# Issuing the last exchange's first round ahead of a residual load, and a bias addition after its second round

## The chip, the core and the metric

The kernel runs on one core of a Trainium2 chip. The metric is device time in microseconds for one execution. TensorE (PE) multiplies matrices, VectorE (DVE), ScalarE (ACT) and GpSimd (POOL) do element-wise work, SyncE (SP) issues DMAs; GpSimd and ScalarE issue some too. Each engine takes its own instructions in order and waits at semaphores for the others.

## The reference, cut to what matters

Eight sequences of 512 tokens by 512 features go through attention with 16 heads of 32, whose queries and keys are shifted by a condition's projections; the input is added to the result.

```python
Q = _split_heads(x @ Wq.T + bq); K = ...; V = ...      # x: (8, 512, 512), 16 heads of 32
tQ = _split_heads(tokens @ Wq.T + bq); tK = ...        # tokens: the condition, one row a sequence
cQ = Q + tQ; cK = K + tK
scores = jnp.einsum('bhqd,bhkd->bhqk', cQ, cK) / jnp.sqrt(jnp.float32(HEAD_DIM))
attn = jax.nn.softmax(scores, axis=-1)
out = jnp.einsum('bhqk,bhkd->bhqd', attn, V)
return x + out.transpose(0, 2, 1, 3).reshape(B, S, D_MODEL)
```

## The kernel before

**Steps.** A step `t` is one sequence (`t // 4`) and four of its heads (`t % 4`), so there are 32, numbered 0 to 31. Work of neighbouring steps is interleaved by hand; nothing reorders it. The framework only adds the semaphore waits that the data need, and it gives the DMAs of SyncE eight semaphores in turn, so that a DMA also waits until the one eight places ahead of it has landed.

**One step.** Scores are computed twice. With queries along the partitions they give the row maxima (VectorE) and, by ScalarE's exponentials, the row sums. With keys along the partitions, and the maxima taken off by a product, they give exponentials that TensorE can multiply with V. For the steps 1 to 29 (`KEPT`) the second form is computed for half of the queries alone. For the other half the exponentials of the first form are kept (`kept[t]`, in the big buffer `store`) and turned: VectorE transposes their 32x32 blocks (`turn_kept`, L660), and then the blocks off the diagonal change places between the four groups of 32 partitions. That is the exchange, `swap_kept(t, move)`, with six pairs of blocks and three rounds of six DMAs of 128 KB:

```python
to, of = [(aside, part(a, g)), (part(a, g), part(g, a)), (part(g, a), aside)][move]
...
(nc.gpsimd if here else nc.sync).dma_start(to, of)     # L682
```

Round 0 copies one block of a pair aside, round 1 moves the other block into its place, round 2 brings the first back. So a pair's round 1 waits for its round 0 to land, and its round 2 for its round 1. For step 29, the last exchange, SyncE issues all of round 0 and the first three pairs of rounds 1 and 2; GpSimd issues the last three pairs of rounds 1 and 2. The prediction calls them first, second and third round. `times_v_half(t, kc, 0, ...)` multiplies the exchanged blocks with V (L840).

**The residual.** `load_residual(t)` issues four DMAs on SyncE (L190), each 64 KB in rows of 32 numbers, into `xr[t]`. `bias_residual(t)` adds V's bias on GpSimd (L203). In `send(t, ...)` VectorE transposes the step's output, GpSimd multiplies by the reciprocals (L913) and adds `xr[t]` (L914), and SyncE stores it (L917).

**The place in the program.** The loop over `thirds(t)` runs up to `t = 28`; in its second third it loads the residual of step 29 and issues that step's first round. Code without a loop follows for steps 29, 30 and 31: the first part, for `t = 29`, holds the second and third round, the row sums' masks (`masked`, L865), the loading of the residual of step 30, and the biases of step 29 and 31. (The last step's residual is already in the core, as `xT`.) Then come the exponentials of step 29's other half, and with `t = 30` `crossed(t, kc, qc)`: scores of step 31 for maxima (L641), maxima and scores of step 30 (L1302, L1305), exponentials on ScalarE (L1320), reductions on VectorE (L1322, L650). After the first `crossed` stands the product of step 29's exchanged blocks, `halves_of(t - 1, banks(2), (0,))`, into a bank that the exponentials of that `crossed` have just emptied; after the second and third stand parts of step 30's own product (`times_v`, L824).

Of the kernel before, what the change touches and what calls it, by code (L numbers as in the profile page):

```python
# [17 lines left out]
def kernel(  # L18
# [112 lines left out]
    def begin(*ws):  # L131
        for w in ws:
            rows = order[w : w + 4]
            pairs = [(j, j + 1) for j in rows if j + 1 in rows]
            last = max(
                pairs, key=lambda p: rows.index(p[0]) + rows.index(p[1]), default=sorted(rows[2:])
            )
            order[w : w + 4] = [j for j in rows if j not in last] + list(last)
        row_of[0] = list(order)
# [22 lines left out]
    def spread(a, d):  # L162

        return a.rearrange("(f j) d -> j f d", j=BL)[:, :, d : d + BL]
# [12 lines left out]
    def turned_by_vector(t):  # L177

        return t < T - 1

    def load_residual(t):

        b, g = divmod(t, G)
        if turned_by_vector(t):
            if t == T - 2:
                xr[t] = late[0][:, 2, :].rearrange("p (f e) -> p f e", e=BL)
            else:
                xr[t] = op.tile([P, NB, BL], F32, tag="xr", name=f"xr_{t}")
            for h in range(HG):
                nc.sync.dma_start(  # L190
                    xr[t][h * BL : (h + 1) * BL], spread(x[b], g * P + h * BL)
                )
        else:

            xr[t] = xT[b][:, g, :]

    def bias_residual(t):

        if turned_by_vector(t):
            bias = bvs[:, t % G, :].unsqueeze(1).broadcast_to([P, NB, BL])  # L200
        else:
            bias = bvl.broadcast_to([P, S])
        nc.gpsimd.tensor_tensor(xr[t], xr[t], bias, ALU.add)  # L203
# [393 lines left out]
    def row_max(t, qc, hold=False, w=HG, scores=True):  # L597

        if t >= T:
            return  # L600
        open_max(t)
        for j in range(HG if scores else 0):
            row_scores(t, qc, j, banks(w + j))
        if row_of[0] or t < T - 2 or t * NS + qc == T * NS - 1:
            for j in range(2) if scores else (1, 0):
                one_max(t, qc, j, banks(w + j))
        else:
            row_max_of(t, qc, 0, banks(w, 2))
        last, both = [banks(w + 2), banks(w + 3)], banks(w + 2, 2)
        apart = row_of[0] and row_of[0][w + 3] - row_of[0][w + 2] > 1  # L610

        def held():
            if apart or hold and t < T - 2:
                for j in range(2):
                    one_max(t, qc, 2 + j, last[j])
            else:
                row_max_of(t, qc, 1, both)

        if hold:
            return held  # L620
        held()
        return nothing
# [4 lines left out]
    def row_max_aside(t, qc):  # L627

        open_max(t)
        for j in range(HG):  # L630
            row_scores(t, qc, j, banks(j))
        nc.scalar.copy(spare, banks(0).rearrange("p (c f) -> p c f", f=P))  # L632
        for j in (1, 2, 3):
            one_max(t, qc, j, banks(j))

    def max_aside(t, qc):
        nc.vector.tensor_reduce(nmax[t][:, qc, 0:1, 0], spare, AX.XY, ALU.max, negate=True)
# [27 lines left out]
    def swap_kept(t, move, some=range(6)):  # L665

        later = 6 if t % 4 == 1 else 2

        def part(a, g):
            return kept[t][a * BL : (a + 1) * BL, g].rearrange("p c h s -> p (c h s)")  # L670

        for n in some:
            a, g = APART[n]
            at = (n + 2) % HG * BL
            aside = (store[:, 6:8] if t == KEPT[-1] else between)[at : at + BL, n // HG]
            aside = aside.rearrange("p i s -> p (i s)")
            to, of = [(aside, part(a, g)), (part(a, g), part(g, a)), (part(g, a), aside)][move]
            if t < KEPT[-1]:
                here = move == 2 or move == 0 and n >= later
            else:  # L680
                here = move > 0 and n >= 3
            (nc.gpsimd if here else nc.sync).dma_start(to, of)  # L682
# [205 lines left out]
    def weighted(t, pt, pd, between):  # L888

        apart = masked(t)
        if t in KEPT:
            of = (0, 2, 1, 3)
            for half in (1, 0):
                for kc in of:
                    times_v_half(t, kc, half, pt, of)
                if half == (t + 1 not in KEPT):
                    spread_sums(apart, pd)
        else:  # L900
            for kc in range(NS):
                times_v(t, kc, pt)
                if kc == (NS - 1 if t + 1 in KEPT else 0):
                    spread_sums(apart, pd)
        rec = reciprocals(t, pd)
        between()
        send(t, pt, rec)
# [237 lines left out]
    def turn_more(t, i, after):  # L1145

        for _ in range((TURNED if t + 1 < KEPT[-1] else TURNED_LAST).get((i, after), 0)):
            if t + 1 in KEPT:
                n = turned[t + 1] = turned.get(t + 1, -1) + 1
                turn_kept(t + 1, n)  # L1150
        even = t % 2 == 0
        if (i, after) == ((2, 1) if even else (0, 2)) or (t, i, after) == (2, 0, 2):
            turn_x(next_x[0])
            next_x[0] += 1

    def thirds(t, made):

        b, r = divmod(t, G)
        of = (t - 1) // G + 1
        begin(0, HG)  # L1160
        turn_more(t, 0, 0)
        row_max_aside(t + 1, 1)
        max_aside(t + 1, 1)
        row_max(t + 1, 2, False, HG)
        turn_more(t, 0, 1)
        denominators(t + 1, 1, None, (1, 2, 3, 0))
        denominators(t + 1, 2, HG)
        weighted(t - 1, banks(0), banks(1), nothing)
        turn_more(t, 0, 2)
        load_blocks(1)  # L1170
        one_item(of, *next(made), (2, 3), ignore, nothing)
        released(0, 1, 4, 5, 7, 6, 2, 3)
        for i in (1, 2):
            begin(HG)
            rows = (t + 1, 3) if i == 1 else (t + 2, 0)
            if i == 1:
                joined(t, i - 1, rows)
                turn_more(t, i, 0)
                row_max(*rows, False, HG, False)
            else:  # L1180
                exponentials_of_rest(t, i - 1)
                turn_more(t, i, 0)
                row_max(*rows, False, HG)
            turn_more(t, i, 1)
            if i == 1:
                first = range(6 if t + 1 < KEPT[-1] else 3)
                swap_kept(t, 2, first)
                split_max(t + 1)
                turn_max(t + 1)
                swap_kept(t, 2, range(len(first), 6))  # L1190
            dens = lambda js=range(HG): denominators(*rows, HG, js)
            n, u, kind = next(made)
            if kind == "first":
                products(of, n, u, kind, False, dens, nothing, None)
                turn_more(t, i, 2)
            elif n == "v":
                small = nothing
                if t + 1 not in KEPT:
                    small = lambda: transpose_max(t + 1, banks(2), nc.scalar.copy)
                other_shared(of, n, u, dens, (0, 3), small, lambda: turn_more(t, i, 2))  # L1200
                released(1, 2, 4, 5, 6, 7, 0, 3)
            else:
                products(of, n, u, kind, False, dens, nothing, False)
                turn_more(t, i, 2)
            if i == 1:
                aparts[t] = masked(t)
            if (t + 1, i) == (KEPT[-1], 1):
                load_residual(t + 1)
                swap_kept(t + 1, 0)
            if i == 2:  # L1210
                if r == 0:
                    combine_x(b + 1, 1, nc.gpsimd)
            else:
                if t > 1:
                    bias_residual(t)
                if r == 0:
                    combine_x(b + 1, 0, nc.gpsimd)
            if i == 2 and t + 1 < KEPT[-1]:
                swap_kept(t + 1, 0)
                load_residual(t + 1)  # L1220
                swap_kept(t + 1, 1)
# [105 lines left out]
    t = T - 3  # L1327
# [11 lines left out]
    else:  # L1339
        row_max_of(t + 1, 2, 1, banks(HG + 2, 2))  # L1340
    row_max_of(t + 1, 2, 0, late[0][:, :2, :])
    bias_residual(t)
    swap_kept(t, 1)
    apart = masked(t - 1)
    aparts[t] = masked(t)
    load_residual(t + 2)
    bias_residual(t + 2)
    swap_kept(t, 2)
    load_residual(t + 1)
    halves_of(t - 1, banks(0), (1,))  # L1350
# [23 lines left out]
    t = T - 2  # L1374
# [25 lines left out]
    t = T - 1  # L1400
# [101 lines left out]
```

## Time and profile before

| what | value |
|---|---|
| median of 3 runs | 649.97 us (649.82 to 650.51) |
| span of the profiled execution | 648.4 us |
| full time of the profiled execution | not given |
| busy: TensorE, VectorE, ScalarE, GpSimd | 99%, 93%, 82%, 63% of the span |
| DMAs within `store` issued by SyncE | 264 of 128 KB, median 2.7 us to landing |
| DMAs within `store` issued by GpSimd | 258 of 128 KB, median 3.8 us to landing |
| loads of `xr` issued by SyncE | 120 of 64 KB, median 4.2 us to landing |

The span runs from the first instruction to the last of one profiled execution. A row of the timeline gives the start in us from the span's start, the time it took, the engine (a q after it: its queue, which only issues), the line of the kernel, the operation and its buffers, and in brackets how long the engine had been idle and who ended that. A row with x6 is six instructions merged. The issuing of a DMA and its landing are different times: the timeline shows the issue.

### The profile page before, as it was taken

The numbers are of one execution on the slowest core, as the hardware profiler recorded it, in microseconds if no ns is written. First come the engines' busy times: TensorE is split into PE (matmuls) and PEld (weight loads), VectorE is DVE, ScalarE is ACT, GpSimd is POOL, SyncE is SP. The second block draws the span as 40 slices with busy tenths as digits, with TensorE's granted clock in tenths as the row PEclk, the third lists the DMA queues.
The fourth block names the chain that finished last, engine by engine and source line by source line (L and its number), as shares of the span: only waits on it lengthen the run. The fifth ranks groups of instructions, "written<-read, shape, count | busy, mean of one in ns | idle before, by whom it ended". The sixth has DMA issues, their size and how long they took to land. (4 is left out here: it accounts for less than half of the span.)

```text
span 648.4 us, 24814 instructions
## 1 busy us (share of the span) xinstructions
PE 641.6 (99%) x9856; PEld 356.7 (55%) x9856; DVE 600.1 (93%) x845; ACT 533.9 (82%) x1364; POOL 410.6 (63%) x651
## 2 busy tenths in 40 slices
PE   9999999999999999999999999999999999999997
PEld 8445555556555555555555555555555555555531
DVE  3799999999999999999999999999999999999887
ACT  2479888889888989888888988898988888898564
POOL 3633655686665776758567776558766576665650
PEclk9999999999999999999999999999999999999999
DMA  7615688878888788977888978788888767797921
GB/s 191 107 27 84 131 164 172 168 169 191 168 171 174 158 182 177 200 156 153 181 178 170 201 154 186 161 175 169 179 193 162 153 144 164 153 188 155 199 48 34
DMA packets 248457, 102.02 MB, mean 157 GB/s; under 512 B 229962, under 2 KB 230474, under 8 KB 248340
## 3 DMA queue, kind: packets, MB, share of 16 engines
q1 hardware_dynamic: 234196, 65.54, 53.6%
q0 software_dynamic: 12384, 33.83, 20.2%
q8 instruction: 78, 1.28, 0.8%
q10 hardware_dynamic: 1760, 1.05, 0.5%
q14 instruction: 39, 0.32, 0.1%
HBM read 19.75 MB, written 8.39 MB: 43 GB/s over the span
## 5 line engine op out<-in xcount | busy, mean ns | idle before, releaser
L593 DVE TENSOR_REDUCE nmax<-psum 128x1 f32<-128x512 f32 x279 | 177.5, 675 | 9.3 <-PE psum L641 4.9
L701 ACT ACTIVATE psum<-psum,nmax 128x512 f32<-128x512 f32 x248 | 165.3, 678 | 3.6 <-DVE nmax L593 3.0
L641 PE MATMUL psum<-kT,qT 32*128 32x512 f32 x1024 | 162.0, 612 | 0.0
L701 ACT ACTIVATE store<-psum,nmax 128x512 f32<-128x512 f32 x204 | 139.6, 701 | 24.9 <-DVE nmax L593 24.7
L682 POOL DMA_DIRECT2D store<-store x258 | 129.0, 504 | 48.9 <-DMA store<-store 31.8
L799 ACT ACTIVATE store<-psum 128x512 f32<-128x512 f32 x232 | 119.8, 602 | 33.2 <-PE psum L785 33.2
L660 DVE STREAM_TRANSPOSE store<-store 128x1024 f32<-128x1024 f32 x116 | 138.9, 1217 | 0.0
L650 DVE TENSOR_REDUCE nmax<-psum 128x2 f32<-128x1024 f32 x98 | 118.8, 1212 | 0.0
L840 PE MATMUL psum<-store,v 128*32 128x256 f32 x1856 | 106.8, 381 | 0.9 <-DMA store<-store 0.9
L840 PEld LDWEIGHTS psum<-store,v 128*32 128x32 f32 x1856 | 57.2, 110 | 57.9 <-ACT wT_q L632 21.2
L913 POOL TENSOR_TENSOR res<-res,recs 128x512 f32<-128x512 f32 x30 | 31.4, 1046 | 89.0 <-DVE res L912 89.0
L785 PE MATMUL psum<-qT,kT 32*128 32x256 f32 x928 | 83.8, 374 | 0.0
L641 PEld LDWEIGHTS psum<-kT,qT 32*128 32x128 f32 x1024 | 61.5, 183 | 35.4 <-issue 17.8
L785 PEld LDWEIGHTS psum<-qT,kT 32*128 32x128 f32 x928 | 60.8, 184 | 5.9 <-issue 0.3
L701 ACT ACTIVATION_READ_ACCUMULATOR psum<-psum,nmax 128x1 f32 x248 | 55.0, 222 | 0.0
L203 POOL TENSOR_TENSOR xr<-xr,bvs 128x512 f32<-128x512 f32 x30 | 38.6, 1285 | 16.4 <-DMA xr<-in_x_dram 15.7
L462 PE MATMUL psum<-wc_v,xc 128*32 128x256 f32 x768 | 47.7, 379 | 0.0
L462 PE MATMUL psum<-xc,wc_q 128*32 128x256 f32 x720 | 44.7, 379 | 0.0
L462 PE MATMUL psum<-xc,wc_k 128*32 128x256 f32 x720 | 44.5, 379 | 0.0
L701 ACT ACTIVATION_READ_ACCUMULATOR store<-psum,nmax 128x1 f32 x204 | 44.3, 217 | 0.0
L914 POOL TENSOR_TENSOR res<-res,xr 128x512 f32<-128x512 f32 x30 | 38.3, 1278 | 2.3
L462 PE MATMUL psum<-xT,wT_k 128*32 128x256 f32 x480 | 34.5, 382 | 0.0
(191 smaller groups left out, 972.4 us busy)
## 6 DMA issues: line engine op xcount, KB each, us to landing
store<-store SPq DMA_DIRECT2D x264, 128.0 KB, 2.7
store<-store POOLq DMA_DIRECT2D x258, 128.0 KB, 3.8
out_dram<-res SPq DMA_DIRECT2D x122, 64.0 KB, 3.7
xr<-in_x_dram SPq DMA_DIRECT2D x120, 64.0 KB, 4.2
x<-in_x_dram SPq DMA_DIRECT2D x112, 64.0 KB, 3.3
w_q<-in_L_cond_Wq_dram SPq DMA_DIRECT2D x4, 256.0 KB, 3.9
w_v<-in_L_cond_Wv_dram SPq DMA_DIRECT2D x16, 64.0 KB, 2.5
w_k<-in_L_cond_Wk_dram SPq DMA_DIRECT2D x16, 48.0 KB, 2.7
```

What stands on the lines that cost most here:

```text
L203: nc.gpsimd.tensor_tensor(xr[t], xr[t], bias, ALU.add)
L462: nc.tensor.matmul(pt[r], still[:, r], moving, start=(kc == kcs[0]), stop=(kc == kcs[-1]))
L593: nc.vector.tensor_reduce(nmax[t][:, qc, j : j + 1, 0], pt, AX.X, ALU.max, negate=True)
L641: nc.tensor.matmul(pt, qkT["q", t][r, qc * P : (qc + 1) * P], qkT["k", t][r, :], start=True, stop=True,)
L650: nc.vector.tensor_reduce(nmax[t][:, qc, pr * 2 : pr * 2 + 2, 0], pt, AX.X, ALU.max, negate=True)
L660: nc.vector.transpose(e, e)
L682: (nc.gpsimd if here else nc.sync).dma_start(to, of)
L701: nc.scalar.activation(to, of, AF.Exp, bias=nmax[t][:, qc, j, :], accum_out=sums[t][:, qc, j, :],)
L785: nc.tensor.matmul(banks(j)[:, i * HS : (i + 1) * HS], qkT["k", t][r, kc * P : (kc + 1) * P], qkT["q", t][r, KQ * P :], start=False, stop= ...
L799: nc.scalar.activation(e[:, j], banks(j), AF.Exp)
L840: nc.tensor.matmul(pt[j * HD : (j + 1) * HD, half * HS : (half + 1) * HS], vs[b % 2][:, kc, (g * HG + j) * HD : (g * HG + j + 1) * HD], e, ...
L914: nc.gpsimd.tensor_tensor(y, y, xr.pop(t), ALU.add)
```

## The change

In `thirds(28)` SyncE issues the six DMAs of step 29's first round before the four of that step's residual, not after them. In the code for step 29 GpSimd adds that residual's bias after both masks and the last step's bias, just before its third round, not before its second.

```diff
             if (t + 1, i) == (KEPT[-1], 1):
+                swap_kept(t + 1, 0)
                 load_residual(t + 1)
-                swap_kept(t + 1, 0)
...
     row_max_of(t + 1, 2, 0, late[0][:, :2, :])
-    bias_residual(t)
     swap_kept(t, 1)
     apart = masked(t - 1)
     aparts[t] = masked(t)
     load_residual(t + 2)
     bias_residual(t + 2)
+    bias_residual(t)
     swap_kept(t, 2)
     load_residual(t + 1)
```

On SyncE, from the store of step 27's output to the load of step 30's residual (`xr_8137` before and `xr_8143` now are step 29's residual; L682 are the exchange's DMAs):

```order
 L917 DMA out_dram<-res_8024 32x16x32 x4
 L727 DMA_TRANSPOSE maxT_8093<-split 128x4x128
-L190 DMA xr_8137<-in_x_dram 32x16x32 x4
-L682 DMA store<-store 32x1024 x12
+L682 DMA store<-store 32x1024 x6
+L190 DMA xr_8143<-in_x_dram 32x16x32 x4
+L682 DMA store<-store 32x1024 x6
 L190 DMA store<-in_x_dram 32x16x32 x4
```

The residual's four issues have moved behind the first six of the exchange, and stand between its first and its second round.

On GpSimd, from the bias of step 28's residual (`xr_7951`) to the third round (`apart` are step 29's masked sums, `xT` the last step's residual):

```order
 L203 TENSOR_TENSOR xr_7951<-xr_7951,bvs 128x512
 L1240 TENSOR_TENSOR v_164<-aside,v_164 128x2x256
-L203 TENSOR_TENSOR xr_8137<-xr_8137,bvs 128x512
 L682 DMA store<-store 32x1024 x3
-L865 TENSOR_TENSOR apart_8234<-sums_7900,which 128x64
+L865 TENSOR_TENSOR apart_8233<-sums_7900,which 128x64
 L203 TENSOR_TENSOR xT<-xT,bvl 128x512
+L203 TENSOR_TENSOR xr_8143<-xr_8143,bvs 128x512
 L682 DMA store<-store 32x1024 x3
```

The bias of step 29's residual has moved from before the second round's three issues to before the third round's; the masks keep their place. TensorE, VectorE and ScalarE keep their order; the waits for two old landings move from VectorE's L1443 to its L1452, to ScalarE's L1442 and to TensorE's L921.

## The prediction

> **What bounds the kernel now.** I read the busy shares, then TensorE's waits over the last 80 us, then the timelines of the engines around the largest one.
>
> ```profile
> span 648.4 us, 24814 instructions
> PE 641.6 (99%) x9856; PEld 356.7 (55%) x9856; DVE 600.1 (93%) x845; ACT 533.9 (82%) x1364; POOL 410.6 (63%) x651
> ```
>
> TensorE is busy 99% of the span, so time is won or lost only where TensorE itself stands still. Its waits from 570 us on:
>
> ```profile
> PE psum L840 <- DMA store<-store: 0.9, 1, 0.9
> PE psum L1454 <- DVE store L1452: 0.5, 1, 0.5
> PE psum L737 <- DVE split L718: 0.2, 1, 0.2
> ```
>
> The longest is a wait for a DMA within `store`: the exchange of step 29's kept blocks, which line 840 multiplies. TensorE's timeline there, and at the two later places where the same pattern (the pair of L1305, then a product) has no DMA in it:
>
> ```profile
> 617.01 0.59 PE L1305 MATMUL psum<-qT,kT 32*128 32x512 f32 x2
> 618.53 1.93 PE L840 MATMUL psum<-store,v 128*32 128x256 f32 x32 [0.93 <-DMA store<-store]
> ...
> 622.06 0.59 PE L1305 MATMUL psum<-qT,kT 32*128 32x512 f32 x2
> 622.58 1.07 PE L824 MATMUL psum<-store,v 128*32 128x512 f32 x8
> ...
> 625.19 0.59 PE L1305 MATMUL psum<-qT,kT 32*128 32x512 f32 x2
> 625.71 1.06 PE L824 MATMUL psum<-store,v 128*32 128x512 f32 x8
> ```
>
> From start to start the undisturbed pattern takes 0.52 us (622.06 to 622.58, 625.19 to 625.71), the disturbed one 1.52. That 0.52 belongs to ScalarE, which must first empty the bank that the product writes:
>
> ```profile
> 616.69 2.07 ACT L1320 ACTIVATE store<-psum 128x512 f32<-128x512 f32 x4 [0.74 <-PE psum L1305]
> 621.74 2.06 ACT L1320 ACTIVATE store<-psum 128x512 f32<-128x512 f32 x4 [0.77 <-PE psum L1305]
> ```
>
> The product starts 0.84 after that line's start at 621.74; at 616.69 the same gives 617.53. So 617.53 is the earliest that the exchange can let line 840 start, and 618.53 - 617.53 = 1.00 us is all that there is to win here.
>
> **Who is late.** GpSimd's queue, with its part of the exchange (L682) and the two bias additions (L203):
>
> ```profile
> 600.95 1.50 POOL L682 DMA_DIRECT2D store<-store  x3 [3.14 <-issue]
> ...
> 603.95 1.28 POOL L1240 TENSOR_TENSOR v<-aside,v 128x512 f32<-128x512 f32 x1
> 605.89 1.27 POOL L203 TENSOR_TENSOR xr<-xr,bvs 128x512 f32<-128x512 f32 x1 [0.66 <-issue]
> 608.84 1.53 POOL L682 DMA_DIRECT2D store<-store  x3 [1.68 <-DMA store<-store]
> 610.38 0.30 POOL L865 TENSOR_TENSOR apart<-sums,which 128x64 f32<-128x64 f32 x1
> 610.64 1.04 POOL L203 TENSOR_TENSOR xT<-xT,bvl 128x512 f32<-128x512 f32 x1
> 611.97 0.55 POOL L682 DMA_DIRECT2D store<-store  x1 [0.29 <-DMA store<-store]
> 613.55 0.49 POOL L682 DMA_DIRECT2D store<-store  x1 [1.02 <-DMA store<-store]
> 614.23 0.49 POOL L682 DMA_DIRECT2D store<-store  x1 [0.20 <-issue]
> ```
>
> The second round starts at 608.84 and waits for the first round to land; the third is issued one by one from 611.97 to 614.23 as the second lands. For that third round the view of its issues gives the time from issue to landing (least, median, most):
>
> ```profile
> DMA to landing us min/median/max: 4.1/4.5/5.1
> ```
>
> 614.23 + 4.1 = 618.33, and 618.53 follows 0.2 later. The chain is first round, second, third, product. Its head is in SyncE's queue (timeline, then the first round alone):
>
> ```profile
> 598.54 1.26 SPq L727 DMA_TRANSPOSE maxT<-split  x1
> 599.85 2.19 SPq L190 DMA_DIRECT2D xr<-in_x_dram  x4
> 602.21 10.28 SPq L682 DMA_DIRECT2D store<-store  x12
> 612.53 3.50 SPq L190 DMA_DIRECT2D store<-in_x_dram  x4
> ...
> L682 SPq DMA_DIRECT2D store<-store x6: 517/714/1355, 602.2 to 606.0; - x6
> DMA to landing us min/median/max: 4.0/4.1/4.4
> ```
>
> **The change, part by part.** *SyncE.* Nothing is added or removed; six issues (first round) pass four (residual). What they need is the last 32x32 transpose of step 29's blocks:
>
> ```profile
> 597.48 2.36 DVE L660 STREAM_TRANSPOSE store<-store 128x1024 f32<-128x1024 f32 x2
> ```
>
> It ends at 599.84; SyncE is free at 598.54 + 1.26 = 599.80. With the 0.17 us that stood between the residual's last issue (599.85 + 2.19 = 602.04) and 602.21, the first round starts at 600.0: 2.2 us sooner. That is the whole gain at the head. *The residual's load* starts when six issues are out: at the median of 0.714 us, 600.0 + 4.3 = 604.3 (at the minimum 603.1, at the pace of the trace, where the sixth starts at 606.0 and takes up to 1.36, 605.2). Its four issues wait, as the order shows, for DMAs eight places ahead; for the last two these are the first round's first two, down by 600.0 + 0.7 + 4.4 = 605.1, which delays nothing. The last of the four starts about 1.7 us after the first, at 606.0. In the trace the load took
>
> ```profile
> L190 SPq DMA_DIRECT2D xr<-in_x_dram x4: 486/496/584, 599.8 to 601.5; - x4
> DMA to landing us min/median/max: 2.8/3.5/4.2
> ```
>
> from issue to landing, so it lands at 606.0 + 3.5 = 609.5 (from 603.1 + 1.7 + 2.8 = 607.6 to 605.2 + 1.7 + 4.2 = 611.1).
>
> *GpSimd.* The second round no longer stands behind the residual's bias (until 605.89 + 1.27 = 607.16) and may start once L1240 ends, at 605.23, and the first round's fourth has landed: 608.84 - 2.2 = 606.6, which I take (605.3 at best, 608.84 if the DMA engines give nothing back). It ends 1.53 later, 608.15; L865 and the last step's bias take 0.3 and 1.04, to 609.5. Now the moved bias comes: 1.27 us from 609.5, when residual and engine are both ready, to 610.8. The third round's three issues, 0.5 each, start at 610.8, 611.3 and 611.8; the second round, by the view of its issues below, lands 2.9 to 3.8 after issue and is down by then, at 607.6 + 3.8 = 611.4 for its last (three issues over 1.53), which the third round's last needs at 611.8. The last lands at 611.8 + 4.5 = 616.3, with 4.1 and 5.1 at 615.9 and 616.9.
>
> ```profile
> DMA to landing us min/median/max: 2.9/3.6/3.8
> ```
>
> All of these lie ahead of 617.53 - 0.2 = 617.33, by 0.4 to 1.4 us. So TensorE's wait goes whole, and ScalarE's line at 616.69 is what it meets next: gain 1.00, not the 2.2 of the head. *Next late* is SyncE's own part of the third round, issued behind its second round:
>
> ```profile
> L682 SPq DMA_DIRECT2D store<-store x3: 507/557/562, 609.8 to 611.9; - x3
> ```
>
> The profile pairs only two of its three landings. Its second round also follows the earlier first round, so it goes forward with it, by up to 2.2; where it did not, it could hold the product at most at today's 618.53.
>
> *Costs taken as nothing.* The bias addition on GpSimd (1.27) passes three issues, L865 and L203; its result and the residual are first read at 623.10, and what it displaces, the third round, is counted above:
>
> ```profile
> 623.10 1.28 POOL L914 TENSOR_TENSOR res<-res,xr 128x512 f32<-128x512 f32 x1
> ```
> After 618.53 the product's followers are TensorE, the copies of ScalarE and VectorE's two reductions:
>
> ```profile
> 618.12 1.21 DVE L650 TENSOR_REDUCE nmax<-psum 128x2 f32<-128x1024 f32 x1
> 621.00 0.25 DVE L1072 RECIPROCAL recs<-den 128x16 f32<-128x16 f32 x1 [1.68 <-ACT den L1067]
> ```
>
> VectorE idles 1.68 us there, more than the 1.00 that it is asked to come forward, and from 621 on each engine waits for TensorE or VectorE only. So the 1.00 reaches the end undiminished. Some waits on landings near the end change places between ScalarE, VectorE and TensorE (L1442, L1443, L921); all are for landings some 30 us old: 0 to 0.1, taken as 0.
>
> **Sum.** 648.4 - 1.0 = 647.4 of span. The profiled execution's full time is not given; if it is like the median run, 649.97 - 648.4 = 1.6 lies around the span, and the forecast is 649.0, 0.15% less. About 0.2% (1.3 us) is what a measurement of this kernel tells from no change; the three runs already spread over 0.69.
>
> **The rivals.**
> *Part of the wait stays* (residual late, or SyncE's third round not sooner): 649.3 to 650.0. It decides where the residual lands after 617.33 - 4.5 - 1.0 - 1.3 = 610.5; my estimate is 609.5, the upper end 611.1.
> *Slower: the moved bias holds the third round.* The same place, further on. GpSimd takes its queue in order, so every microsecond of the residual beyond 610.5 moves the product. At 611.5 the gain is gone; for 0.2% more time it has to land after 612.8. That is 6.8 us after an issue at 606.0, where the rows give 4.2 at most. Then 651.3 or more.
> *Step 28's third round is slowed.* GpSimd issues it from 600.95 (first row of its fence), now among SyncE's first round instead of the residual's small rows. In the present trace it landed at most 3.5 us after issue:
>
> ```profile
> DMA to landing us min/median/max: 2.4/3.0/3.5
> 607.44 1.93 PE L840 MATMUL psum<-store,v 128*32 128x256 f32 x32
> ```
>
> TensorE needs it at 607.44. The last of three, issued near 601.96, may take 5.2 us before TensorE waits. Beside other traffic step 29's took up to 5.1, so I see 0 to 0.5 us lost: 649.0 to 649.5. The Trainium skill (DMA: Bandwidth & Descriptors, Queues, rings and completion order) says that each DMA engine takes the queues in turn, packet by packet, so that transfers of SyncE and GpSimd slow each other. The trace agrees in kind (3.5 at most there, 5.1 among other transfers); by the rule the sum would be this rival's, between 649.0 and 649.5.
> *More than the profile shows*: the wait is for DMAs, and the executions spread over 0.69 us; where an ordinary one waits 0.5 longer than the profiled one, the gain is 1.5: 648.4.
>
> **How the numbers follow.** Forecast 649.0: 0.55. More gain, 648.4: 0.20. Part of the wait stays: 0.13. Step 28 slowed: 0.05. Slower, 651.3: 0.07. Faster by over 0.2% is the second of these alone, 0.20; slower 0.07; the rest, 0.73, is within 0.2%. The range runs from 648.4 to 650.1: it leaves out the slower case and some of the larger gain, and takes in a gain of nothing (649.97).
>
> **What would show it.** Right: the first round on SyncE starts near 600.0 and the residual near 604; GpSimd's second round near 606.6, before both bias additions, its third near 611 in one piece; the product of line 840 starts 0.5 after the last pair of L1305, with no DMA wait. Wrong: a wait of line 840 for a DMA that remains, at 618 or new at 607, or GpSimd idle ahead of its residual bias past 610.5.

## The result, and the profile after

| | runs | median, us | ratio to before, 95% interval |
| --- | --- | --- | --- |
| before, as shown to the prediction | 3 | 649.97 | |
| before, beside the changed kernel | 21 | 650.29 | |
| changed kernel | 21 | 649.54 | 0.9986 [0.998, 0.9992] |
| changed kernel, again | 11 | 649.78 | 0.9994 [0.9986, 1.0003] |
| changed kernel, a third time | 11 | 649.84 | 0.9989 [0.998, 0.9998] |

The change saves about 0.1%: the three ratios average 0.9990, which is 0.7 us of 650. Two of the three intervals leave out 1. The gain lies within the 0.2% that the prediction called no change. The profiled execution of the changed kernel took 649.67 us. First its page (span, busy shares), then TensorE's waits from 570 us on:

```profile
span 647.8 us, 24814 instructions
PE 641.7 (99%) x9856; PEld 357.3 (55%) x9856; DVE 600.3 (93%) x845; ACT 533.5 (82%) x1364; POOL 409.9 (63%) x651
...
PE psum L1454 <- DVE store L1452: 0.5, 1, 0.5
PE psum L840 <- ACT store L1320: 0.2, 1, 0.2
PE psum L737 <- DVE split L718: 0.2, 1, 0.2
```

The 0.9 us wait of L840 for a DMA is gone from the list, and 0.2 us is left under another name. TensorE's timeline at that product, and ScalarE's line that sets its floor:

```profile
617.12 0.59 PE L1305 MATMUL psum<-qT,kT 32*128 32x512 f32 x2
617.95 1.29 PE L840 MATMUL psum<-store,v 128*32 128x256 f32 x20 [0.24 <-ACT store L1320]
...
616.80 2.07 ACT L1320 ACTIVATE store<-psum 128x512 f32<-128x512 f32 x4 [0.74 <-PE psum L1305]
```

From the last pair of L1305 to the product it is now 0.83 us (617.12 to 617.95), against 1.52 before and 0.52 undisturbed. The name in the bracket isn't the cause: 616.80 + 0.84 = 617.64, so ScalarE was done 0.31 before the product started. What was late was still the exchange. SyncE's queue (timeline, then the last three of its exchange issues):

```profile
599.15 1.21 SPq L727 DMA_TRANSPOSE maxT<-split  x1
600.53 4.13 SPq L682 DMA_DIRECT2D store<-store  x6
604.70 3.32 SPq L190 DMA_DIRECT2D xr<-in_x_dram  x4
608.07 6.54 SPq L682 DMA_DIRECT2D store<-store  x6
...
L682 SPq DMA_DIRECT2D store<-store x3: 508/536/1759, 611.6 to 612.8; - x3
```

GpSimd's queue (timeline, then the time from issue to landing, least, median and most, of its third round and of that round's last issue alone):

```profile
606.94 1.08 POOL L682 DMA_DIRECT2D store<-store  x2 [1.70 <-DMA store<-store]
609.45 0.49 POOL L682 DMA_DIRECT2D store<-store  x1 [1.43 <-DMA store<-store]
609.96 0.30 POOL L865 TENSOR_TENSOR apart<-sums,which 128x64 f32<-128x64 f32 x1
610.21 1.04 POOL L203 TENSOR_TENSOR xT<-xT,bvl 128x512 f32<-128x512 f32 x1
611.21 1.28 POOL L203 TENSOR_TENSOR xr<-xr,bvs 128x512 f32<-128x512 f32 x1
612.44 1.52 POOL L682 DMA_DIRECT2D store<-store  x3
...
DMA to landing us min/median/max: 4.0/4.2/4.4
...
L682 POOL DMA_DIRECT2D store<-store x1: 492/492/492, 613.5 to 613.5; - x1
DMA to landing us min/median/max: 4.0/4.0/4.0
```

The first round starts 1.7 us sooner than before (602.21 to 600.53), GpSimd's second 1.9 sooner, and its third goes out in one piece, its last issue at 613.5 instead of 614.23. That one is down by 613.5 + 4.0 = 617.5. SyncE's third round, on the other hand, is later than before: last issue 612.8 (611.9 before), and that issue alone takes 1.76 us, to 614.6. With ScalarE done by 617.64 and GpSimd's part down by 617.5, it is what the product at 617.95 waited for. The views pair no landing with that issue, but in the trace the last update of its semaphore comes at 617.81, the last of all three.

### The profile page after: what moved, and what is told of

Its sections match the earlier page's. It is cut to its first block, busy times and chain, and to the rows that moved or that the text cites. A ratio compares the mean times of both kernels' runs of the same rounds, so it can differ in the third digit from the quotient of the medians.

```text
span 647.8 us, 24814 instructions
## 1 busy us (share of the span) xinstructions
PE 641.7 (99%) x9856; PEld 357.3 (55%) x9856; DVE 600.3 (93%) x845; ACT 533.5 (82%) x1364; POOL 409.9 (63%) x651
## 5 line engine op out<-in xcount | busy, mean ns | idle before, releaser
L682 POOL DMA_DIRECT2D store<-store x258 | 128.6, 503 | 47.2 <-DMA store<-store 28.8
L840 PE MATMUL psum<-store,v 128*32 128x256 f32 x1856 | 106.8, 381 | 0.2 <-ACT store L1320 0.2
L840 PEld LDWEIGHTS psum<-store,v 128*32 128x32 f32 x1856 | 57.3, 110 | 57.2 <-ACT wT_q L632 21.2
```

The source lines that it names most:

```text
L840: nc.tensor.matmul(pt[j * HD : (j + 1) * HD, half * HS : (half + 1) * HS], vs[b % 2][:, kc, (g * HG + j) * HD : (g * HG + j + 1) * HD], e, ...
```

## The experiments

Diffs are against the kernel before, except in the last two, which start from the changed kernel.

**How each is read.** The start of a profiled execution varies: the first product of the steady part (L772) starts between 74.6 and 75.5 us, whatever the kernel. So I take, of each, the stretch from there to the end of the last VectorE instruction. For the changed kernel:

```profile
74.79 0.40 PE L772 MATMUL psum<-maxT,onesb 3*128 3x512 bf16 x4
...
643.92 0.76 DVE L1462 TENSOR_TENSOR store<-psum,rec 128x256 f32<-128x256 f32 x2
```

643.92 + 0.76 - 74.79 = 569.89. For the kernel before it is 644.50 + 0.76 - 74.67 = 570.59. The table has it for all executions, beside the distance from L1305 to the product of step 29 and any wait of TensorE that the kernel before doesn't have. The wait of 1.54 is 1.84 from instruction to instruction at step 28's product where the others have 0.30. The rest are waits of L737: at the earlier of its two places (614 to 616 us) the whole wait, which the kernel before doesn't have, at the later one (627 to 629) what exceeds the usual 0.2. The last column is 569.60 + (distance - 0.51) + other waits, where 569.60 is the stretch of the two executions of the changed kernel that show no such wait.

| kernel | L1305 to L840 | other new waits | stretch | by the sum |
| --- | --- | --- | --- | --- |
| before | 1.52 | | 570.59 | 570.61 |
| before, again | 0.92 | | 570.04 | 570.01 |
| before, a third time | 1.43 | | 570.53 | 570.52 |
| changed kernel | 0.83 | | 569.89 | 569.92 |
| changed kernel, again | 0.51 | | 569.59 | 569.60 |
| changed kernel, a third time | 0.51 | | 569.60 | 569.60 |
| first round alone | 2.05 | 0.70 | 571.91 | 571.84 |
| bias alone | 1.79 | | 571.06 | 570.88 |
| no exchange of step 29 | 0.51 | | 569.61 | 569.60 |
| residual last | 0.51 | 0.3 | 569.95 | 569.90 |
| residual by GpSimd | 0.51 | 1.54 | 571.15 | 571.14 |
| bias after the third round | 0.51 | 1.1 | 570.76 | 570.70 |
| residual last, biases later | 0.51 | 0.6 | 570.25 | 570.20 |

**Both kernels again.** The same program, profiled once more, is the control for everything below.

> The kernel of before, unchanged, as a control: time within 0.1% of before; in its trace the gap from the last L1305 to L840 is 1.2 to 1.8 us (1.52 in the first trace), with a wait for a DMA within store. If the gap of one and the same program varies by a microsecond, the gain read from two traces says little.

> The changed kernel, unchanged, as a control on the same chip: 0.05 to 0.2% less than before; in its trace the gap L1305 to L840 is 0.5 to 1.0 us (0.83 in the first trace).

> The kernel before, unchanged, for one more profiled execution. Theory (the wait at step 29's product ends with a landing whose time varies from execution to execution): the distance L1305 to L840 is between 0.9 and 1.6 us, neither at the floor of 0.51 nor the same as either of the two seen (1.52, 0.92). Rival (the first profile was an outlier): 0.9 to 1.0 again.

> The changed kernel, unchanged, once more. Theory: the distance L1305 to L840 is between 0.5 and 0.9 us, ratio 0.9980 to 0.9995. Rival (no gain beyond the noise): a ratio whose interval holds 1.0 in its middle half.

TensorE's timeline at the product, for before again, before a third time, changed again, changed a third time:

```profile
617.10 0.59 PE L1305 MATMUL psum<-qT,kT 32*128 32x512 f32 x2
618.03 1.29 PE L840 MATMUL psum<-store,v 128*32 128x256 f32 x20 [0.34 <-ACT store L1320]
```

```profile
617.39 0.59 PE L1305 MATMUL psum<-qT,kT 32*128 32x512 f32 x2
618.82 1.93 PE L840 MATMUL psum<-store,v 128*32 128x256 f32 x32 [0.83 <-ACT store L1320]
```

```profile
617.12 0.59 PE L1305 MATMUL psum<-qT,kT 32*128 32x512 f32 x2
617.64 1.72 PE L840 MATMUL psum<-store,v 128*32 128x256 f32 x28
```

```profile
616.99 0.59 PE L1305 MATMUL psum<-qT,kT 32*128 32x512 f32 x2
617.51 1.93 PE L840 MATMUL psum<-store,v 128*32 128x256 f32 x32
```

One program's distance differs by up to 0.6 us between executions: 1.52, 0.92 and 1.43 before (mean 1.29), 0.83, 0.51 and 0.51 after (mean 0.62). So the 1.2 to 1.8 expected of before again missed (0.92); the 0.9 to 1.6 expected of its third execution held, and 0.92 was no rule. The brackets name ScalarE here too, but in all three executions of before the product starts 0.2 us after the last of GpSimd's third round has landed, at 618.34, 617.83 and 618.62 by the last updates of its semaphore. The difference of the means, 0.67, agrees with the measured 0.7, and the stretches say the same: mean 570.39 before, 569.69 after, 0.70 less. That they agree so closely is in part luck: each mean is of three, and two of the six (before again, 649.64; changed a third time, 649.14) have the lowest time of their eleven runs. The timed ratio of the control "before, again" to before was 1.0005 [0.9997, 1.0014], so a kernel measured against itself can come out 0.05% off.

**One half alone.** First the first round moved and the bias left ahead of the second round:

```diff
             if (t + 1, i) == (KEPT[-1], 1):
-                load_residual(t + 1)
                 swap_kept(t + 1, 0)
+                load_residual(t + 1)
```

> SyncE issues the first round ahead of the residual, but GpSimd still adds the residual's bias ahead of its second round. Theory (the chain first round, second, third, product; GpSimd in order): in the changed kernel the residual is issued at 604.7 to 608.0 us and GpSimd's bias addition follows at 611.2, so here the second round can only start near 612.4 instead of 606.9, the third near 616 to 617, and the product of line 840 near 620 to 621.5: a gap of 3 to 4.5 us from the last L1305 to L840, and 1.5 to 3 us more than before. Rival (the earlier first round alone carries the gain): the gap is near 0.8 us as in the changed kernel, and the time 0.6 to 1.0 us less than before.

Measured: 653.32 us median of 5, ratio 1.0041 [1.0027, 1.0054], a clear loss. Timelines of GpSimd, VectorE and TensorE:

```profile
610.58 1.27 POOL L203 TENSOR_TENSOR xr<-xr,bvs 128x512 f32<-128x512 f32 x1 [4.66 <-DMA xr<-in_x_dram]
611.79 1.52 POOL L682 DMA_DIRECT2D store<-store  x3
613.58 1.04 POOL L203 TENSOR_TENSOR xT<-xT,bvl 128x512 f32<-128x512 f32 x1
...
613.74 0.94 DVE L715 CAST split<-nmax 128x16 bf16<-128x16 f32 x1
...
615.53 0.40 PE L737 MATMUL psum<-identb,split 128*128 128x128 bf16 x4 [0.70 <-DVE split L718]
620.53 1.93 PE L840 MATMUL psum<-store,v 128*32 128x256 f32 x32 [1.46 <-DMA store<-store]
```

GpSimd stands 4.66 us for the later residual, and its second round, queued behind the bias, starts at 611.79, some 2.3 us later than before's 608.84 (this execution starts 0.7 later). The distance was forecast at 3 to 4.5 us and is 2.05: the second round starts earlier than the 612.4 that I expected, and the last L1305 itself comes some 0.8 later in the execution, behind L737's wait for a CAST of VectorE that took 0.94 us (see the last section). Then the bias alone:

```diff
-    bias_residual(t)
     swap_kept(t, 1)
...
     bias_residual(t + 2)
+    bias_residual(t)
     swap_kept(t, 2)
```

> Only the bias addition moves behind the second round; SyncE's order is that of before. Theory: the second round waits for the first round's landing at 608.8 us whether the bias is ahead of it or not, and the last of the third round is issued near 614.2 as before, so the gap L1305 to L840 stays 1.3 to 1.8 us and the time within 0.3 us of before. Rival (GpSimd's queue was the cause and the bias alone carries the gain): second round earlier than 608, gap 0.5 to 0.9 us, time 0.6 to 1.0 us less than before.

Measured: ratio 1.0002 [0.9993, 1.0011], no difference. Timelines of GpSimd and VectorE:

```profile
610.07 1.52 POOL L682 DMA_DIRECT2D store<-store  x3 [4.09 <-DMA store<-store]
...
612.85 1.26 POOL L203 TENSOR_TENSOR xr<-xr,bvs 128x512 f32<-128x512 f32 x1
614.07 1.52 POOL L682 DMA_DIRECT2D store<-store  x3
...
613.86 0.33 DVE L715 CAST split<-nmax 128x16 bf16<-128x16 f32 x1
```

With the bias out of its way the second round still waits, 4.09 us, for the first to land (610.07 here; this execution starts 0.8 later than the profile of before, so 609.3 against 608.84). The bias had cost the second round nothing; ahead of the third it costs 1.27. (The CAST takes 0.13 more than its usual 0.20, too little for a wait in the list; it is most of the 0.18 that the sum lacks in the table.) So neither half gains. The first makes the residual late for the bias, and the second takes the bias out of that wait. Only both together save anything. What the account leaves open: the first half's median lies 1.2 us above the execution that was profiled (652.15), and three of the other four took 653.3 to 653.8, so they lost more, at a place that I have no profile of.

**How much is there to win, and does it arrive?** Step 29's exchange left out (so its products use blocks that were not exchanged), and then all three rounds ahead of the residual and the bias behind them:

```diff
-                swap_kept(t + 1, 0)
...
-    swap_kept(t, 1)
...
-    swap_kept(t, 2)
```

> The kernel of before without the exchange of step 29: its three rounds, 18 DMAs of 128 KB, are left out, so that step 29's blocks are multiplied where they lie. This measures the ceiling. Theory: the product then waits for ScalarE alone, 0.52 us after the last L1305 and 0.84 after the start of ScalarE's L1320, so 1.0 us less than before (0.7 to 1.3), and nothing else gets faster. Rival (the exchange's traffic also slows other work at the end): more than 1.5 us less.

```diff
-                load_residual(t + 1)
...
-    bias_residual(t)
     swap_kept(t, 1)
...
     swap_kept(t, 2)
+    load_residual(t)
     load_residual(t + 1)
+    bias_residual(t)
```

> The residual of step 29 is loaded after all three rounds on SyncE and its bias added after the third round on GpSimd. Theory: SyncE's third round then stands four issues (about 3 us) earlier and lands well before 617.3 us, so the rest of the wait that the changed kernel shows (0.83 from L1305 to L840, floor 0.52) goes too: gap 0.5 to 0.6 us, time about 1.0 us less than before and 0.3 less than the changed kernel (0 to 0.6). Rival (the rest of the wait is ScalarE's, as the wait view names it): gap stays near 0.8 us, time as the changed kernel's.

Measured: 1.0001 [0.9992, 1.001] and 1.0000 [0.9991, 1.0009]. Both bring the product to the floor of 0.51, and neither was faster in time: both forecasts of 1.0 us less missed. Without the exchange the stretch is 569.61, the full 1.0 less than before's first profile, but that kernel then takes 3.65 us from the last VectorE instruction to the end of its span, where the kernel before takes 3.10 (648.36 - 645.26). Half a microsecond is lost in the ending, for a reason that I didn't find, and the remaining gain of 0.2 (569.61 + 0.55 against before's mean of 570.39) lies inside the interval. With the residual last the stretch is 0.4 less than before's mean, which the interval also holds; the rest is given back behind the product. Both were profiled in executions below their medians (649.92 of 650.34, 649.61 of 650.26), so whether the others lose more elsewhere stays open. The timelines with the residual last (GpSimd, VectorE, TensorE):

```profile
617.26 1.27 POOL L203 TENSOR_TENSOR xr<-xr,bvs 128x512 f32<-128x512 f32 x1 [5.11 <-DMA xr<-in_x_dram]
624.44 2.37 POOL L1276 TENSOR_TENSOR acc<-store 128x1024 f32<-128x1024 f32 x1
...
626.36 0.50 DVE L715 CAST split<-nmax 128x16 bf16<-128x16 f32 x1
...
627.64 0.40 PE L737 MATMUL psum<-identb,split 128*128 128x128 bf16 x4 [0.50 <-DVE split L718]
```

The late bias pushes GpSimd's accumulation until it overlaps VectorE's small CAST of L715, which takes 0.50 us instead of 0.20, and TensorE's L737 waits 0.50 instead of 0.20.

**The residual in another place.** GpSimd loads it, in its idle time ahead of step 28's third round, and adds the bias ahead of the second round as before:

```diff
-    def load_residual(t):
+    def load_residual(t, queue=nc.sync):
...
                 turn_max(t + 1)
+                if t + 1 == KEPT[-1]:
+                    load_residual(t + 1, nc.gpsimd)
                 swap_kept(t, 2, range(len(first), 6))
...
-                load_residual(t + 1)
                 swap_kept(t + 1, 0)
```

> SyncE issues the three rounds without the residual between them; GpSimd loads the residual of step 29 in the 3.1 us in which it idles before 600.9, and adds its bias ahead of the second round, while it waits for the first round's landing. Theory (both parts of the third round must land by 617.3, SyncE's too): gap L1305 to L840 at the floor of 0.52 to 0.6 us, no new wait, and 0.7 to 1.0 us less than before; 0.3 less than the changed kernel. Rival (GpSimd needs much longer to issue a load of 512 short rows, so that step 28's third round is late for the product at 607.4): a new wait at the product of line 840 at 607 and a time as before or more.

Measured: ratio 1.0023 [1.0014, 1.0033], slower, as the rival had it. GpSimd's timeline, the time to landing of these three DMAs of step 28's third round, then TensorE's timeline at step 28's product:

```profile
599.91 2.62 POOL L190 DMA_DIRECT2D xr<-in_x_dram  x4 [1.92 <-issue]
602.52 1.49 POOL L682 DMA_DIRECT2D store<-store  x3
...
DMA to landing us min/median/max: 4.4/5.0/5.4
...
609.30 1.93 PE L840 MATMUL psum<-store,v 128*32 128x256 f32 x32 [1.47 <-issue]
```

Step 29's product is at the floor, but the four issues take 2.62 us and push step 28's third round from 600.95 to 602.52, and it now takes up to 5.4 us to land, where it took 3.5 before. TensorE waits at step 28's product, which starts at 609.30 instead of 607.44 (of the difference, 0.3 is this execution's later start). This is the place that the prediction's third rival named, reached by another way.

**The bias behind the third round.** The changed kernel with GpSimd's bias after the exchange's last issue, to see whether the bias is what leaves the 0.3 us:

```diff
     bias_residual(t + 2)
-    bias_residual(t)
     swap_kept(t, 2)
     load_residual(t + 1)
+    bias_residual(t)
```

> The changed kernel, but GpSimd adds the residual's bias after its third round. Theory (the rest of the wait in the changed kernel is SyncE's third round, last landing by 617.8): GpSimd's third round is issued no later than 612.5, yet the gap stays 0.7 to 0.9 us; and the bias addition, now at about 613 to 614.3, meets VectorE's CAST of line 715 at 613.1, which then takes until GpSimd's addition ends (0.3 to 1.3 us in place of 0.2), so that TensorE waits for VectorE before L737: time 0.3 to 1.0 us more than the changed kernel. Rival (GpSimd's third round is what the product still waits for): gap 0.5 to 0.6, time 0.3 less than the changed kernel.

Measured: 1.0000 [0.9991, 1.0009]. The product is at the floor, and the gain is gone (GpSimd, VectorE, TensorE):

```profile
613.33 1.28 POOL L203 TENSOR_TENSOR xr<-xr,bvs 128x512 f32<-128x512 f32 x1
...
613.32 1.37 DVE L715 CAST split<-nmax 128x16 bf16<-128x16 f32 x1
...
615.53 0.40 PE L737 MATMUL psum<-identb,split 128*128 128x128 bf16 x4 [1.12 <-DVE split L718]
```

The bias now meets the earlier of the two CASTs, which takes 1.37 us for 0.20, and TensorE waits 1.12 at L737. The CAST came as expected; the distance of 0.7 to 0.9 that I expected did not (0.51). As a test of what limits the product it decides nothing: the changed kernel reached the floor in two of three executions without it. Last, the version that should avoid both collisions:

```diff
                 swap_kept(t + 1, 0)
-                load_residual(t + 1)
...
     bias_residual(t + 2)
-    bias_residual(t)
     swap_kept(t, 2)
+    load_residual(t)
     load_residual(t + 1)
...
     send_sums(t - 1, whole[t - 1], den)
-    bias_residual(t + 1)
+    bias_residual(t)
...
     sum_of(t, acc, 1, nc.gpsimd, [1])
+    bias_residual(t)
```

> Steps 29 and 30 issue their three rounds on SyncE first and the residual behind them; GpSimd adds step 29's bias behind the evictions of step 28's last part and step 30's bias behind step 29's last accumulation, so that no bias stands ahead of a third round and none meets the CAST of L715 at the two products. Theory (the wait at step 29's product is whatever lands last of the third rounds, and the CAST is held only by a GpSimd operation under way): the distance L1305 to L840 of step 29 is at the floor, 0.5 to 0.6 us, both CASTs in this stretch take 0.20 us, and the time is 0.7 to 1.0 us less than before's, 0 to 0.3 less than the changed kernel's (ratio 0.9985 to 0.999). Rival (a saved wait at this product is given back at a later place whatever is done, as with the two kernels that reached the floor and gained nothing): the distance is at the floor and the time is before's, ratio 0.9995 to 1.0005, with a new TensorE wait of 0.3 us or more behind the product.

Measured: 0.9996 [0.9987, 1.0005]; the account's 570.25 against before's mean of 570.39 would be 0.9998. It missed, by my own placing (GpSimd, VectorE, TensorE):

```profile
626.29 1.27 POOL L203 TENSOR_TENSOR store<-store,bvs 128x512 f32<-128x512 f32 x1
...
626.83 0.80 DVE L715 CAST split<-nmax 128x16 bf16<-128x16 f32 x1
...
628.40 0.40 PE L737 MATMUL psum<-identb,split 128*128 128x128 bf16 x4 [0.80 <-DVE split L718]
```

Step 30's bias, put behind the accumulation, runs into the second CAST. The rival's words "given back whatever is done" fit the time, but not its reason: the changed kernel's other two executions keep the whole of it. No kernel that ran was better than the changed one.

## Why the prediction was right, point by point

- **The bound and the ceiling held.** TensorE's wait at step 29's product is the one thing that moved, ScalarE's L1320 is the floor (0.51 in six kernels), and what is won there reaches the end of the stretch: over 13 executions it follows that distance and the named extra waits to within 0.2 us, mostly 0.07. In the measured time the gain shows for the changed kernel alone.
- **The size came from one sample.** The ceiling of 1.00 was right for the profiled execution, yet before's distance from L1305 to the product was 0.92, 1.43 and 1.52 in three. The gain is 0.7, not 1.0. I gave 0.20 to ordinary executions that wait longer than the profiled one; of the two others seen, both wait less. That 649.0 came so near is in part luck: the ceiling was read from the longest of the three, and the range took in no change at all.
- **The head.** The first round started at 600.53 and 600.10 and 600.46 in the three executions, where I said 600.0. Good to half a microsecond.
- **GpSimd's second round was mis-sized.** Forecast 606.6 for its start (606.94), but "it ends 1.53 later" failed: its third issue waits another 1.43 us, to 609.45, for SyncE's sixth DMA of the first round to land. I had timed the round by the fourth landing alone. In the profile of before that wait cannot be seen: the round started later there, and its three issues follow each other without a wait. The bias thus ran at 611.21, not 609.5, and the third round at 612.44, not 610.8. At 617.5 its last landing was just in time, 1.2 later than the forecast 616.3.
- **The residual was not what held the bias, but it was late.** The last of its four issues started 2.2 us after the first (604.7 to 606.9), not 1.7, and ended at 608.0. Forecast to land at 609.5, it landed at 611.03 by the last update of its semaphore in the trace (609.9 and 609.8 in the other two executions): near the upper end of 611.1, and past the 610.5 that was to leave part of the wait. It cost nothing in that execution because GpSimd, itself 1.7 late, came to the bias only at 611.21. That two delays of much the same size hid each other is luck. Had the residual gone past, the first-round-only kernel shows the price: the slower rival's mechanism is real (4.66 us of waiting), but it needed the bias ahead of the second round.
- **"Next late" was the right name with the wrong sign.** I let SyncE's second and third rounds go forward with the first. They stand behind the residual's four issues in the same queue, and went back: the last issue from 611.9 to 612.8, and its landing, at 617.81, past the floor of 617.64. That left 0.31 us of the wait in the first profile (the rival "part of the wait stays", and the sign of being wrong that the prediction names) and nothing in the other two, where the last issue started at 611.9 and 613.3 and landed at 616.3 and 617.4.
- **Step 28's third round was slowed, and it cost nothing.** It landed at most 4.2, 3.8 and 4.0 us after issue in the three executions, against 3.5, 3.7 and 3.6 before, and its product started at 607.54, without a wait: less than the 5.2 that it could take. The runs agree in kind with the rule that the prediction cites from the Trainium skill (DMA: Bandwidth & Descriptors, Queues, rings and completion order).
- **The level.** 649.0 against 649.54: 0.3 us is the ceiling above, and 0.3 the sample of three runs (649.97; 650.29 in 21). Around the span lie 1.9 us (649.67 - 647.8), not 1.6.

## What to carry to other kernels

An issue that is moved ahead on an in-order queue moves what it passes behind it: follow the passed issues, and everything queued after them, to their last landing. A wait that ends with a DMA landing is a sample, so profile the same program two or three times before its length is taken as the ceiling of a gain. And idle time on GpSimd isn't free where a short VectorE operation on the path falls into it.

## What the runs showed of the hardware

- **A small VectorE CAST is held by a GpSimd addition beside it.** L715 (128x16, float32 to bfloat16) takes 0.20 us alone. In five kernels it met a GpSimd addition (under way, or in one case starting within 0.02 us of it) and took 0.33, 0.50, 0.80, 0.94 and 1.37, each time ending 0.05 to 0.08 us after that addition did (bias after the third round: 614.69 and 614.61). The Trainium skill (SBUF — State Buffer, Who interferes with whom) says that VectorE in a 2-port mode and GpSimd contend for a shared port pair, and the later one blocks fully; the runs agree, though none shows which mode the CAST is in. In the changed kernel the bias ends at 612.49 and the CAST starts at 613.12, so the bias has 0.63 us of room before it eats into the gain. The prediction did not look at this.
- **GpSimd's issue of a residual load took 0.65 us each** (2.62 for four), against 0.49 to 0.52 for the exchange's DMAs in the same timeline.
- **The time at which the exchange's DMAs land moves this kernel by 0.6 us from one execution to the next** (570.59, 570.04 and 570.53 for the kernel before), in a stretch where everything else repeats to 0.1.
